# The second remainder in the split of B is made by GpSimd

## The chip, the cores and the metric

The kernel runs on one core of one Trainium2 chip. The metric is the time of one execution on the device in microseconds (us), as a median of several runs. A core has TensorE (PE in the profile, its weight loads PEld), VectorE (DVE), ScalarE (ACT), GpSimd (POOL) and SyncE (SP), which here only issues DMA transfers. Each engine works through its own queue in order; semaphores hold an instruction until the work of another engine that it needs is done.

## The reference

Four layers follow each other on four images of 64 x 64 positions and 96 channels. The first two are selective scans, the last two a linear attention with a small feed-forward part in quantised arithmetic. Nearly all of the time is in the first two. Of one of these, cut to what matters:

```python
x_dbl = jnp.einsum('bkdl,kcd->bkcl', xs, x_proj_weight)          # 4 directions k of each image
dts, Bmat, Cmat = jnp.split(x_dbl, [DT_RANK, DT_RANK + D_STATE], axis=2)
delta = jax.nn.softplus(jnp.einsum('bkrl,kdr->bkdl', dts, dt_projs_weight) + bias)
def step(h, inp):                                                # along l, 4096 positions
    u_l, dl, b_l, c_l = inp
    dA = jnp.exp(dl[..., None] * A)
    h = dA * h + (dl * u_l)[..., None] * b_l[:, :, None, :]      # 192 channels x 16 states
    y = jnp.einsum('bkdn,bkn->bkd', h, c_l)
    return (h, y)
```

B is a row for each of the 16 states, shared by all channels. Each channel's scan of state n needs the product of delta, u and B's row n.

## The kernel before

The images are taken in pairs. For each layer and pair, `scan_pair` runs four directions, in each four chunks of T = 1024 positions, and in each chunk three steps j: the first 128 channels of image 0, those of image 1, and a shared step (j = 2) with the last 64 channels of both. A step has 16 states, in eight groups of NG = 2. So a pair has 48 steps, the whole run 192, with 3072 scans of 128 x 1024.

For a group, ScalarE makes `da` = exp(delta x A) a group ahead (`start_ahead`). The product du x B comes in one of three ways, which the strings OWN and SHARED choose for each state. V: TensorE spreads B's row over 128 partitions into PSUM (`bp`, two buffers) with a selection matrix `sel`, and VectorE multiplies by `du`. A: ScalarE makes the product with time on the partitions (`x`), and TensorE turns it. G: GpSimd multiplies `du` by a copy of B that a transfer has spread (`dbu`), and the exponential goes to PSUM. Then VectorE scans (lines 659 to 666), GpSimd copies the last states (line 672) and multiplies each `h` by C (`cb`, line 674), and TensorE adds up over the states in `yp`, three groups later (LAG).

All instructions of the loop go through the helper at line 71, which keeps the order of the program on each engine. So the order of the calls in Python is the order in each queue, and the profile gives line 71 for all of them; rows are told apart by their tiles.

The work that prepares the next chunk is written as generators. `project` makes B, C and the input of delta for the chunk to come, and `drive` lets it go on at fixed places: `yield 2, 10` means in step j = 2, after the scans of the group that starts with state 10. The matmul that spreads B (way V) takes bfloat16. To keep the precision, B is split into three bfloat16 parts whose sum is B: `parts[0]` is B rounded, `rest` = B - `parts[0]` is the first remainder, `parts[1]` is `rest` rounded, and `parts[2]` = `rest` - `parts[1]` is the second remainder (line 385). Tiles: `parts` is 128 x 8 x 3 x 32 in bfloat16 and `rest` 128 x 8 x 32 in float32, both in SBUF with one buffer. Both are used once in three steps. The places are:

- (2, 8): ScalarE copies B out of PSUM to `bt` and rounds it to `parts[0]`; VectorE makes `rest` from PSUM and `parts[0]`
- (2, 10): ScalarE rounds `rest` to `parts[1]`, and at the same place the second remainder is made
- (2, 12): TensorE turns the parts in eight transposes (`bpps`)
- (2, 14): ScalarE copies them to `bparts`, which the next chunk's V states read

The 64 uses of `project` are 60 inside the loops and four at the openings of the pairs, where the chain runs on its own. The last step of each pair prepares nothing.

Of the kernel before, what the change touches and what calls it, by code (L numbers as in the profile page):

```python
# [21 lines left out]
ALU = mybir.AluOpType  # L22
# [308 lines left out]
def scan_pair(tc, pk, cst, ident, u, first_weights, layer, pr):  # L331

    nc = InOrder(tc)
    par, amat, dsum, w, y = layer.par, layer.amat, layer.dsum, layer.w, layer.y[pr]
    with ExitStack() as stage:
# [17 lines left out]
        def project(k, uv):  # L353


            wx = weights[k][0]
            bparts = p2.tile([NP, T], BF16, name="bparts")
            cdt = p2.tile([NC, T], F32, name="cdt")
            crow = pd.tile([ND, T], F32, name="crow")
            bt = p2.tile([128, T // 128, 2 * NS], F32, name="bt")  # L360
            projected.append((uv, bparts, crow, cdt, bt))
            for hf in range(2):
                for j in range(3):
                    yield hf, 8 + 2 * j
                    if j == 0:
                        ps = pm.tile([NC, 512], F32, name="xps", tag="m1")
                    nc.tensor.matmul(ps, wx[:, j], uv[j][:, 8 * hf : 8 * hf + 8], start=(j == 0), stop=(j == 2))
                yield hf, 14
                nc.scalar.copy(cdt[:, 512 * hf : 512 * hf + 512], ps)
            nc.sync.dma_start(out=crow, in_=cdt[:ND])  # L370
            yield 2, 6
            ps = pm.tile([128, T // 128, 2 * NS], F32, name="btps", tag="m1")
            for t in range(T // 128):
                nc.tensor.transpose(ps[:, t], cdt[BR, 128 * t : 128 * t + 128], ident[BR, BR])

            parts = p2.tile([128, T // 128, 3, 2 * NS], BF16, name="parts", bufs=1)
            rest = p2.tile([128, T // 128, 2 * NS], F32, name="rest", bufs=1)
            yield 2, 8
            nc.scalar.copy(bt, ps)
            nc.scalar.copy(parts[:, :, 0], ps)  # L380
            nc.vector.tensor_tensor(rest, ps, parts[:, :, 0], ALU.subtract)
            yield 2, 10
            nc.scalar.copy(parts[:, :, 1], rest)
            yield 2, 10
            nc.vector.tensor_tensor(parts[:, :, 2], rest, parts[:, :, 1], ALU.subtract)
            yield 2, 12
            ps = pm.tile([NP, T], BF16, name="bpps", tag="m1")
            for t in range(T // 128):
                nc.tensor.transpose(
                    ps[:, 128 * t : 128 * t + 128], parts[:, t].rearrange("p s n -> p (s n)"), ident16  # L390
                )
            yield 2, 14
            nc.scalar.copy(bparts, ps)
            yield None
# [46 lines left out]
        def begin_project(k, ci):  # L441
            tr, c = chunk_of(k, ci)
            return project(k, [part(t, tr, c) for t in u])
# [549 lines left out]
```

## Time and profile before

| | |
|---|---|
| time, median of 3 runs | 10827.77 us (10821.13 to 10835.91) |
| span of the profiled execution | 10818.7 us |
| granted TensorE clock, mean | 0.886 |
| scan loops of the four pairs | about 2300 to 2309 us each, 9214 us in all |
| scans on VectorE | 3072, 2.3 us each |
| multiplies of h by C on GpSimd | 3072, 2.37 us each |
| second remainder on VectorE | 64, 1.35 us each on average |

The scan loops are 85% of the span. Busy shares of the whole run mix them with the stages between the pairs and with the last two layers, so a stretch of a loop is what to read. A row of a group gives the engine, the operation, the tiles written and read, the shape and the number, then busy time and the mean of one. Idle time before an instruction is put down to the work that ended last before it.

### The profile page before, as it was taken

How to read it: one execution, taken by the hardware profiler on the slowest of the kernel's cores; microseconds unless marked ns; L12 is line 12 of the kernel's file. 1: busy time of each engine (PE TensorE's matmuls, PEld its weight loads, DVE VectorE, ACT ScalarE, POOL GpSimd, SP SyncE). 2: the span in 40 equal slices, each digit the busy share in tenths (PEclk: the TensorE clock that was granted, in tenths of full speed). 3: DMA queues.
4: the chain of work that ended last, by engine and by line, in shares of the span. 5: the costliest groups of instructions: out<-in, count | busy, mean ns of one | idle time of the engine just before them, and what ended most of it. 6: DMA issues, size and time to landing. Idle time of an engine off the chain costs nothing. (4 is left out here: it accounts for less than half of the span.)

```text
span 10818.7 us, 143079 instructions
## 1 busy us (share of the span) xinstructions
PE 8073.8 (75%) x48032; PEld 5963.0 (55%) x48032; DVE 9699.3 (90%) x6962; ACT 8758.7 (81%) x18679; POOL 9001.7 (83%) x5242
## 2 busy tenths in 40 slices
PE   7777777777777777777777777777777777777666
PEld 4555555554555555555555555555455555555544
DVE  7999999997899999998799999999699999999655
ACT  6888888885888888886688888888588888888556
POOL 3999999992899999996599999999299999999544
PEclk9899899988898998998898999999899989898766
DMA  4677777775677777776577777777467777777600
GB/s 123 205 210 217 213 225 217 218 216 138 199 212 209 219 218 218 220 215 193 149 209 210 212 218 221 217 218 213 136 206 213 212 215 222 218 216 214 184 3 25
DMA packets 960471, 2114.16 MB, mean 195 GB/s; under 512 B 413526, under 2 KB 704664, under 8 KB 762008
## 3 DMA queue, kind: packets, MB, share of 16 engines
q1 hardware_dynamic: 959736, 2105.01, 67.7%
q8 instruction: 381, 6.24, 0.2%
q14 instruction: 354, 2.90, 0.1%
HBM read 1943.27 MB, written 161.48 MB: 195 GB/s over the span
## 5 line engine op out<-in xcount | busy, mean ns | idle before, releaser
L71 POOL TENSOR_TENSOR h<-h,cb 128x1024 f32<-128x1024 f32 x3072 | 7198.4, 2367 | 268.9 <-issue 77.4
L71 DVE TENSOR_TENSOR_SCAN h<-da,last,bp 128x1024 f32<-128x1024 f32 x2064 | 4735.9, 2335 | 132.2 <-PE bp L71 15.1
L71 ACT ACTIVATE x<-dut,bt 128x128 f32<-128x128 f32 x12288 | 3495.3, 370 | 0.8 <-PE bp L71 0.5
L71 PE MATMUL yp<-ident,h 128*128 128x128 f32 x24576 | 3324.6, 295 | 9.8 <-POOL h L71 9.8
L71 PEld LDWEIGHTS yp<-ident,h 128*128 128x128 f32 x24576 | 3151.3, 155 | 126.4 <-issue 75.4
L71 ACT ACTIVATE da<-delta,amat 128x1024 f32<-128x1024 f32 x2752 | 3063.9, 1138 | 173.1 <-DVE h L71 172.9
L71 PE MATMUL bp<-ident,x 128*128 128x128 f32 x10240 | 1652.4, 312 | 1319.9 <-DVE h L71 920.8
L71 PEld LDWEIGHTS bp<-ident,x 128*128 128x128 f32 x10240 | 1333.4, 160 | 1880.0 <-ACT x L71 1046.2
L71 DVE TENSOR_TENSOR bp<-du,bp 128x1024 f32<-128x1024 f32 x1472 | 1779.2, 1213 | 230.3 <-PE bp L71 228.2
L71 DVE TENSOR_TENSOR_SCAN h<-da,bp 128x1024 f32<-128x1024 f32 x688 | 1537.7, 2274 | 48.8 <-ACT da L71 8.1
L71 PE MATMUL bp<-bparts,sel 96*128 96x512 bf16 x2944 | 922.5, 396 | 831.4 <-DVE h L71 810.4
L71 PEld LDWEIGHTS <-sel 96*128 96x128 bf16 x2944 | 224.3, 100 | 1640.5 <-DVE h L71 1030.3
L71 ACT ACTIVATE bp<-delta,amat 128x1024 f32<-128x1024 f32 x320 | 358.1, 1119 | 536.9 <-DVE h L71 535.5
L71 POOL TENSOR_TENSOR dbu<-du,bb 128x1024 f32<-128x1024 f32 x320 | 754.9, 2359 | 0.0
L71 POOL TENSOR_TENSOR du<-delta,u 128x1024 f32<-128x1024 f32 x192 | 506.8, 2640 | 202.3 <-ACT delta L71 176.5
L81 POOL TENSOR_TENSOR ln_rs<-ln_ve,half 128x4 f32<-128x4 f32 x64 | 83.9, 1311 | 596.0 <-DVE ln_ve L79 494.6
L71 DVE TENSOR_TENSOR_SCAN h<-bp,last,dbu 128x1024 f32<-128x1024 f32 x240 | 558.7, 2328 | 16.8 <-POOL dbu L71 13.1
L71 PE MATMUL xps<-u,wx 128*76 128x512 f32 x768 | 561.0, 820 | 5.7 <-ACT cdt L71 2.9
L71 POOL COPY last<-h 128x2 f32<-128x2 f32 x1152 | 223.0, 194 | 396.3 <-DVE h L71 394.4
L71 ACT ACT_TABLE_LOAD x384 | 492.7, 1283 | 7.1
L71 PE MATMUL dps<-cdt,wdt 12*128 12x512 f32 x768 | 448.0, 664 | 0.1
L71 ACT COPY dut<-dups 128x512 f32<-128x512 f32 x384 | 220.9, 575 | 255.0 <-PE dups L71 255.0
(132 smaller groups left out, 6439.4 us busy)
## 6 DMA issues: line engine op xcount, KB each, us to landing
cb<-crow SPq DMA_DIRECT2D x1024, 1024.0 KB
cb<-crow SPq DMA_DIRECT2D x1024, 512.0 KB
bb<-crow SPq DMA_DIRECT2D x384, 256.0 KB
bb<-crow SPq DMA_DIRECT2D x128, 512.0 KB
y<-ysum SPq DMA_DIRECT2D x192, 256.0 KB
kept<-y SPq DMA_DIRECT2D x160, 256.0 KB
y<-ysum SPq DMA_DIRECT2D x64, 512.0 KB
zt<-zg SPq DMA_DIRECT2D x64, 384.0 KB
```

The source lines that it names most:

```text
L71: return self.tc.keep_in_program_order(getattr(self.engine, op)(*args, **kwargs))
L81: nc.gpsimd.tensor_tensor(rs, ve, half, ALU.pow)
```

## The change

The second remainder, `parts[2]`, is subtracted by GpSimd rather than VectorE. The place in the program stays the same, and so do the tiles. It is meant to take a short instruction, and the wait ahead of it, out of VectorE's queue. In GpSimd's queue it stands after the multiplies of the group before (states 8 and 9) and ahead of the copy and the multiplies of states 10 and 11. The order on TensorE and ScalarE is as before.

```diff
             nc.scalar.copy(parts[:, :, 1], rest)
             yield 2, 10
-            nc.vector.tensor_tensor(parts[:, :, 2], rest, parts[:, :, 1], ALU.subtract)
+            nc.gpsimd.tensor_tensor(parts[:, :, 2], rest, parts[:, :, 1], ALU.subtract)
             yield 2, 12
```

## The prediction

> **What bounds the kernel now.** I read the page's first part, then the waits of each engine, then the stretch of one scan pair, then the two remainders themselves. The page's chain of waits is of no use here: its shares add up to 5% of the span, all in the attention and feed-forward layers at the end, so it never reaches the scans. First the page, the share of the span that each engine is busy:
>
> ```profile
> PE 8073.8 (75%) x48032; PEld 5963.0 (55%) x48032; DVE 9699.3 (90%) x6962; ACT 8758.7 (81%) x18679; POOL 9001.7 (83%) x5242
> ```
>
> Busy times by stretch, here the scan loop of the first image pair (the other three pairs have 2302 to 2309 us and the same loads within 0.3%):
>
> ```profile
> 180.00:2480.00 2300.00, 1726.12 (x10630) 1307.87 (x10630) 2182.34 (x1161) 1976.18 (x4244) 2143.85 (x1180) 0.90 0.75 214
> ```
>
> The columns are PE, PEld, DVE, ACT, POOL. In the loop VectorE is busy 94.9%, GpSimd 93.2%, ScalarE 85.9%. VectorE leads and GpSimd is close behind, so who waits for whom decides:
>
> ```profile
> DVE bp L71 <- PE bp L71: 228.2, 262, 11.8
> ...
> DVE rest L71 <- ACT parts L71: 56.5, 4, 24.5
> ...
> DVE parts L71 <- ACT parts L71: 52.0, 52, 1.5
> ...
> DVE h L71 <- POOL dbu L71: 28.0, 27, 1.8
> ```
>
> ```profile
> POOL last L71 <- DVE h L71: 394.4, 279, 11.8
> ```
>
> VectorE waits for GpSimd 28 us in the whole run; GpSimd waits for VectorE's scans 394 us. So the scans on VectorE set the pace, and what is taken out of VectorE's queue in the loop is worth nearly its time. The instructions on the tiles of the split (min, median, max in ns):
>
> ```profile
> L71 DVE TENSOR_TENSOR rest<-btps,parts x64: 396/399/426, 154.1 to 9956.7; 128x256 f32<-128x256 f32 x64
> L71 ACT CAST parts<-rest x64: 385/389/406, 154.5 to 9963.8; 128x256 bf16<-128x256 f32 x64
> L71 DVE TENSOR_TENSOR parts<-rest,parts x64: 424/1096/3250, 155.0 to 9964.5; 128x256 bf16<-128x256 f32 x64
> ```
>
> Both subtractions have the same 128x256 shape, but the second takes up to eight times the first. One instance in order of time, VectorE and then GpSimd:
>
> ```profile
> 440.75 2.33 DVE L71 TENSOR_TENSOR_SCAN h<-bp,last,dbu 128x1024 f32<-128x1024 f32 x1
> 444.41 2.46 DVE L71 TENSOR_TENSOR parts<-rest,parts 128x256 bf16<-128x256 f32 x1 [1.33 <-ACT parts L71]
> 446.80 1.22 DVE L71 TENSOR_TENSOR bp<-du,bp 128x1024 f32<-128x1024 f32 x1
> ```
>
> ```profile
> 443.97 0.18 POOL L71 COPY last<-h 128x2 f32<-128x2 f32 x1
> 444.23 4.87 POOL L71 TENSOR_TENSOR h<-h,cb 128x1024 f32<-128x1024 f32 x2
> 452.70 0.18 POOL L71 COPY last<-h 128x2 f32<-128x2 f32 x1 [3.60 <-DVE h L71]
> ```
>
> VectorE ends scan 11 at 443.08, waits 1.33 us for ScalarE's cast, and then the subtraction lies in its record for 2.46 us while GpSimd multiplies. GpSimd then idles 3.60 us, waiting for the scans that came late.
>
> **What the Trainium skill says.** "SBUF — State Buffer", section "Who interferes with whom": a VectorE instruction with two inputs in SBUF contends with a GpSimd instruction that reads SBUF, one with at most one SBUF input does not. The trace agrees: the first remainder (one input in PSUM) never exceeds 426 ns; the second (both in SBUF) takes 424 ns in the four openings, where GpSimd is idle, and 1.41 us on average in the loop. VectorE's other work in the loop has one input in PSUM: du by bp, and the scans, which read da or dbu beside bp. "GPSIMD Engine Reference", "Elementwise — side-by-side cycle accounting": 4497 ns for a two-input fp32 instruction of 2048 elements, 2.20 ns each; the trace's 1024-element multiply has 2367 ns, 2.31 each. "Perfetto Trace Analysis", "Optimizing Scalar/DVE Operations": offloading between these two engines might not help because of the shared port; here the contended operation is the very one that moves.
>
> **The change, part by part.**
>
> Removed from VectorE: 64 subtractions, 86.1 us by their group row (1345 ns mean). Four are in the openings of the pairs, where nothing else runs (4 x 0.42 = 1.7 us). The 60 in the loop are 84.4 us, or 1.41 each. The wait ahead of them goes too: 52.0 us, 0.87 each. An instruction's record reaches about 0.07 us into the next one (444.41 + 2.46 - 446.80), so 1.41 + 0.87 - 0.07 = 2.21 us each, 132 us. A second way gives the same: from the start of scan 11 to the start of scan 12 the 60 steps take 5.72 us on average, and the last step of each pair, which prepares no projection, takes 3.55 us four times out of four. 2.17 x 60 = **130 us**, which I use.
>
> What VectorE meets when it arrives 2.2 us earlier: its next work, du by bp for state 12, needs bp from TensorE. That buffer was freed by scan 10 at 443.0 - 2.3 = 440.8, and the two matmuls ran then. In the last steps of the pairs VectorE does go straight on. da for states 12 and 13 is on ScalarE ahead of the cast. So nothing stands directly behind the removed instruction.
>
> Given back later: the loop has 60 stalls of different size (0.43 to 4.5 us), a small experiment of its own. Regressing the time from state 12 to state 0 of the next step on the size of the stall gives -0.13 us for each us: a longer stall is partly made up, mostly at states 13 to 14, where VectorE waits for TensorE's bp. A whole step later the slope is -0.3, but with noise of 1.2 us. Around three more steps later it is lost in the noise. I take 18% given back: 130 x 0.82 = 107 us.
>
> Added to GpSimd: 64 subtractions of 256 elements. The trace has none on GpSimd. Lower bound 256 x 2.20 = 0.56 us from the page of the skill; upper 1.2 us, if the 2-byte, strided operand doubled the 0.59 us that 2.31 ns give. I take 0.7 us, the 0.59 plus part of the 0.27 us from the start of the small copy to the next multiply. In the loop 60 x 0.7 = 42 us. It comes ahead of the copy of the last states and the two multiplies of states 10 and 11. It waits for the cast, which ends 0.74 us after scan 11 on average; GpSimd reaches that point 0.86 us after scan 11 on average, so the wait is seldom over 1 us, and mostly where GpSimd would otherwise wait for scan 11. Behind it are the two multiplies, for which TensorE's adding-up waits three groups later. Today GpSimd starts the first of them 2.4 us on average after scan 11; with 0.7 more it lags about 3 us. A group costs it 0.19 + 2 x 2.37 = 4.9 us, VectorE 5.8 (state 12, 13) and 6.9 (14, 15), so the lag is gone by the next step. On the whole, a pair's GpSimd load becomes 2144 + 15 x 0.7 = 2155 us of about 2273, 95%. It stays off the path, and I cost it at **nothing**; VectorE's scans hide it.
>
> Moved: TensorE's eight transposes of parts wait for GpSimd rather than VectorE. They are queued ahead of bp for states 14 and 15. Today they start 5.4 us after scan 11 on average, and never under 3.2; GpSimd ends at about max(0.74, 0.86) + 0.7 = 1.6 us after scan 11, at worst about 3. Hidden behind TensorE's earlier work in its queue (the sums and the transposes of du), at no cost. The copy to bparts follows as before.
>
> The four openings: 0.7 instead of 0.42 us in a serial chain, 4 x 0.3 = +1 us. Outside the scans nothing changes. Sum: -107 + 1 = -106, **10,722 us**, -1.0%.
>
> **The rivals.**
>
> *All of it stays* (no give-back): 10,828 - 130 + 1 = 10,699. For it: the last steps of the pairs show 3.55 us exactly. Against: the slope.
>
> *Half is lost.* GpSimd at 95% has spikes: the step of the shared channels has three dbu products, 16 x 2.37 + 3 x 2.36 + 2.64 + 8 x 0.19 = 49 us of GpSimd, against 50.9 from start to start now and 48.8 once the stall is gone. If its lag grows until dbu comes late or TensorE's queue stands behind parts, about 1 us of each 2.2 comes back: 10,828 - 60 = 10,768. Against: the next two steps have one dbu each, 44 us against 46.2 and 46.8 from start to start.
>
> *No change:* ScalarE (86%) becomes the pace, because its casts, 16 scalings and table loads are what VectorE waited for at the cast. 10,828. Against: ScalarE itself waits 535 us for scans to free bp.
>
> *Slower:* the wait for the cast holds GpSimd at the head of its queue, the lag passes to TensorE, which stands at the transposes of parts with bp of states 14 and 15 behind, and VectorE loses 3 us where it gained 2.2: 60 x 0.8 = 48, 10,876. Against: 5.4 - 1.6 = 3.8 us of margin on average.
>
> **How the numbers follow.** The forecast with its give-back 0.58, all stays 0.12, half lost 0.17, no change 0.05, slower 0.08. The likeliest gives 10,722. The range goes from 10,688 (132 us and a few tenths of a per cent of measuring noise and idle) to 10,782 (half lost, with GpSimd's subtraction at 1.2 us): what is left out below and above is under 2 in 10. Faster by over 0.2%: 0.87; within: 0.05; slower: 0.08.
>
> **What would show it.** VectorE's busy time down by 86 us, its wait for ScalarE's parts down to the 56 us of the first remainder. Scan 11 to scan 12 in the shared step at about 3.55 us. Sixty GpSimd subtractions of 0.6 to 1.2 us; GpSimd's wait for scans down from 394 us. A scan loop of about 2275 us. Wrong if GpSimd's record is well over 1.2 us, if VectorE's wait for dbu or bp grows by more than 25 us, or if TensorE now waits for parts.

## The result and the profile after

The changed kernel takes 10,766.4 us (median of 6 runs, 10,753.4 to 10,773.7) against 10,826.5 us before (6 runs). The ratio is 0.9943, with a 95% interval of 0.9931 to 0.9956: 60 us less. The direction is as forecast and the size a little over half of the 106 us. Each experiment below has its ratio to runs of the kernel before that were made with it (medians of 10,823 to 10,826 us), so a difference of a few us between two experiments says nothing.

First the page after, the busy share of each engine:

```profile
PE 8109.9 (75%) x48032; PEld 6016.2 (56%) x48032; DVE 9622.5 (89%) x6898; ACT 8754.9 (81%) x18679; POOL 9028.9 (84%) x5306
```

VectorE lost 77 us of busy time and 64 instructions, GpSimd gained 27 us. The row of the second remainder in the view of the tile (min, median, max in ns):

```profile
L71 POOL TENSOR_TENSOR parts<-rest,parts x64: 661/673/695, 153.2 to 9908.1; 128x256 bf16<-128x256 f32 x64
```

On GpSimd it is 0.68 us, evenly. The waits of VectorE after the change (us in total, times, longest), and the one of GpSimd that answers to that shown before:

```profile
DVE bp L71 <- PE bp L71: 301.9, 332, 13.1
...
DVE rest L71 <- ACT parts L71: 53.9, 4, 24.5
...
DVE h L71 <- POOL dbu L71: 24.1, 23, 2.1
```

```profile
POOL last L71 <- DVE h L71: 338.3, 238, 11.8
```

The wait for the cast is gone from VectorE's list; what is left of ScalarE's parts there is the first remainder in the four openings. VectorE's wait for GpSimd's dbu did not grow (28.0 to 24.1). But its wait for TensorE's bp rose from 228.2 to 301.9 us, and that is the surprise. The instance shown before, now in the changed kernel, on VectorE:

```profile
438.03 2.34 DVE L71 TENSOR_TENSOR_SCAN h<-bp,last,dbu 128x1024 f32<-128x1024 f32 x1
440.29 1.21 DVE L71 TENSOR_TENSOR bp<-du,bp 128x1024 f32<-128x1024 f32 x1
441.60 4.59 DVE L71 TENSOR_TENSOR_SCAN h<-da,last,bp 128x1024 f32<-128x1024 f32 x2
446.91 2.36 DVE L71 TENSOR_TENSOR bp<-du,bp 128x1024 f32<-128x1024 f32 x2 [0.73 <-PE bp L71]
```

and on GpSimd:

```profile
442.82 0.68 POOL L71 TENSOR_TENSOR parts<-rest,parts 128x256 bf16<-128x256 f32 x1
443.44 0.19 POOL L71 COPY last<-h 128x2 f32<-128x2 f32 x1
443.71 4.69 POOL L71 TENSOR_TENSOR h<-h,cb 128x1024 f32<-128x1024 f32 x2
448.35 0.18 POOL L71 COPY last<-h 128x2 f32<-128x2 f32 x1
```

After scan 11 VectorE goes straight on. Four instructions later, at the product for state 14, it waits 0.73 us for TensorE. GpSimd works without a gap.

Where the time went is read best from the start of one scan to the start of the next. I took these from the scan rows of the timeline and averaged over all 64 steps of a kind. The profile also records which share of its full clock TensorE was granted; "half clock" is the time in records of 0.5, per step, between the starts of those states (in the last row over the 60 places where a step follows inside the same pair).

| | before | after | change x 64 |
|---|---|---|---|
| shared step, scan 11 to 12 | 5.59 us | 3.56 us | -130 us |
| shared step, 13 to 14 | 4.57 us | 5.23 us | +42 us |
| next step (image 0), 1 to 2 | 4.33 us | 4.70 us | +24 us |
| step of image 1, 1 to 2 | 3.94 us | 4.09 us | +10 us |
| four scan loops in all, first scan's start to last scan's end | 9224 us | 9175 us | -50 us in all |
| half clock, states 11 to 14 of the shared step | 6.72 us | 6.60 us | |
| half clock, state 15 to state 2 of image 0's step | 4.61 us | 6.68 us | |

The 130 us came as forecast. 76 of them were given back at three places, all of them waits for TensorE. The profiled spans differ by 57 us; the 7 us that are not in the loops have no cause that I know.

### The profile page after: what moved, and what is told of

Its sections match the earlier page's. It is cut to its first block, busy times and chain, and to the rows that moved or that the text cites. A ratio compares the mean times of both kernels' runs of the same rounds, so it can differ in the third digit from the quotient of the medians.

```text
span 10761.8 us, 143139 instructions
## 1 busy us (share of the span) xinstructions
PE 8109.9 (75%) x48032; PEld 6016.2 (56%) x48032; DVE 9622.5 (89%) x6898; ACT 8754.9 (81%) x18679; POOL 9028.9 (84%) x5306
## 5 line engine op out<-in xcount | busy, mean ns | idle before, releaser
L71 PE MATMUL bp<-ident,x 128*128 128x128 f32 x10240 | 1679.8, 316 | 1288.9 <-DVE h L71 938.7
L71 PEld LDWEIGHTS bp<-ident,x 128*128 128x128 f32 x10240 | 1361.0, 163 | 1852.8 <-ACT x L71 1025.7
L71 DVE TENSOR_TENSOR bp<-du,bp 128x1024 f32<-128x1024 f32 x1472 | 1780.6, 1214 | 303.3 <-PE bp L71 301.9
L71 ACT COPY ysum<-yp 128x1024 f32<-128x1024 f32 x192 | 194.4, 1012 | 288.9 <-PE yp L71 288.9
```

What stands on the lines that cost most here:

```text
L71: return self.tc.keep_in_program_order(getattr(self.engine, op)(*args, **kwargs))
```

## Experiments

**Does GpSimd take it back?** Nothing makes the third part any more; it is zeroed once for each pair.

```diff
         weights = {0: first_weights}
+        parts = p2.tile([128, T // 128, 3, 2 * NS], BF16, name="parts", bufs=1)
+        nc.gpsimd.memset(parts, 0.0)
...
-            nc.gpsimd.tensor_tensor(parts[:, :, 2], rest, parts[:, :, 1], ALU.subtract)
```

> Leaves the second remainder out on both engines: the third part of B is set to zero once for each pair and never made again, so the output is slightly less precise and the time shows what the subtraction on GpSimd costs. Theory TensorE (what came back after the change, +0.66 us at states 13 to 14 and +0.37 us at states 1 to 2 of the next step, is TensorE's queue, which starts at half clock): the time stays at 10,760 to 10,770 us, within 5 us of the changed kernel. Rival GpSimd (the 0.7 us in GpSimd's queue, and its wait for the cast, delay the multiplies and what waits for them): about 40 to 49 us less, 10,720 us.

10,767.7 us, ratio to before 0.9949 (0.9936 to 0.9961), the same as the changed kernel. States 13 to 14 take 5.26 us and states 1 to 2 of image 0's step 4.70, as with the subtraction. So the subtraction on GpSimd, and the order that it forces there, cost nothing that these runs can tell, and the rival GpSimd falls.

**Was it the shared port?** In the kernel before, `rest` moves from SBUF to PSUM, into one tile with B.

```diff
-            ps = pm.tile([128, T // 128, 2 * NS], F32, name="btps", tag="m1")
+            both = pm.tile([128, 2, T // 128, 2 * NS], F32, name="btps", tag="m1")
+            ps, rest = both[:, 0], both[:, 1]
...
-            rest = p2.tile([128, T // 128, 2 * NS], F32, name="rest", bufs=1)
```

> The kernel before, with the second remainder still on VectorE, but with the first remainder kept in PSUM, so that the subtraction has one input in SBUF only. Theory shared port (the time over 0.42 us was contention with GpSimd): its record falls from 1.35 us to 0.42 to 0.5 us on average, the wait for the cast stays at about 50 us in all, scan 11 to scan 12 falls from 5.7 to about 4.8 us, and the time falls by 40 to 60 us, to about 10,775 us. Rival (the long records have another cause, such as the strided 2-byte operand or a late semaphore): the record stays over 1 us and the time within 10 us of before.

The rows of the two remainders in the view of the tile, where `btps` is now B and `rest` together:

```profile
L71 DVE TENSOR_TENSOR btps<-btps,parts x64: 405/406/433, 153.8 to 9921.0; 128x256 f32<-128x256 f32 x64
L71 DVE TENSOR_TENSOR parts<-btps,parts x64: 396/425/426, 154.7 to 9928.5; 128x256 bf16<-128x256 f32 x64
```

The same subtraction of the same shape, still on VectorE, into the same strided 2-byte tile, falls from up to 3250 ns to 426 ns at most. So what was long was the second SBUF input beside a busy GpSimd, as the Trainium skill's "SBUF — State Buffer" ("Who interferes with whom") states. Its wait for the cast stays (46.6 us in 44 times). Scan 11 to 12 takes 4.58 us, and states 13 to 14 stay at 4.61, so nothing is given back there; states 1 to 2 of the next two steps give back 18 us. The time is 10,771 us, 0.9949 (0.9937 to 0.9962): this edit removes one of the two microseconds of the stall and brings about as much as the change that removes both. So the second microsecond is worth little. How little stays open: 5 us by the medians, 16 by the loops of the two profiled executions (9191 and 9175 us), and that of this edit was the slowest of its five.

**What holds TensorE up?** TensorE's queue between bp for state 13 and bp for state 14, before and then after the change:

```profile
443.23 1.94 PE L71 MATMUL bp<-ident,x 128*128 128x128 f32 x8 [1.30 <-DVE h L71]
444.96 3.08 PE L71 MATMUL yp<-ident,h 128*128 128x128 f32 x16
447.88 0.60 PE L71 MATMUL dups<-ident,du 128*128 128x128 f32 x4
448.32 0.61 PE L71 MATMUL bpps<-ident,parts 128*96 128x128 bf16 x8
450.45 0.60 PE L71 MATMUL bp<-bparts,sel 96*128 96x512 bf16 x2 [1.53 <-DVE h L71]
```

```profile
440.51 1.94 PE L71 MATMUL bp<-ident,x 128*128 128x128 f32 x8 [1.37 <-DVE h L71]
442.25 3.31 PE L71 MATMUL yp<-ident,h 128*128 128x128 f32 x16
445.39 0.60 PE L71 MATMUL dups<-ident,du 128*128 128x128 f32 x4
445.83 0.61 PE L71 MATMUL bpps<-ident,parts 128*96 128x128 bf16 x8
446.28 1.03 PE L71 MATMUL bp<-bparts,sel 96*128 96x512 bf16 x4
```

Before, TensorE came to bp for state 14 and waited 1.53 us for VectorE; after, it goes straight through, and VectorE waits for it. Both chains begin at the end of scan 11, which frees the buffer for bp 13. Averaged over the 60 places, in us after that moment:

| | before | after |
|---|---|---|
| TensorE: bp 13 done | 2.09 | 2.09 |
| sums done | 5.08 | 5.09 |
| transposes of du done | 5.58 | 5.56 |
| bp 14 starts | 6.28 | 5.85 |
| VectorE: scan 13 done | 7.96 | 5.79 |
| scan 14 starts | 10.22 | 8.75 |

TensorE's work did not move by more than 0.02 us up to the transposes of du. VectorE used to come 1.7 us after bp 14 had started, and now comes 0.06 us before it starts. The stretch is slow in TensorE because it begins at half clock: 16 transposes of the sums take 3.1 to 3.3 us here, and 1.91 us at full clock. Over the whole changed kernel these transposes, within a run, follow each other every 213 ns inside records of 0.5 and every 109 ns inside records of 1.0. Ahead of the stretch TensorE idles in the group with state 11, whose bp ScalarE makes, until bp for state 12 (here after the change):

```profile
438.17 0.97 PE L71 MATMUL bp<-bparts,sel 96*128 96x512 bf16 x2 [3.28 <-DVE h L71]
```

The Trainium skill, "TensorE: Matmul & The Clock Gate", "What's actually happening", says that the throttled clock is the default and that activity releases it. The trace agrees, and the length of a single pause is not what counts. The clock records here hold 1.0 and 0.5 and change on a grid of 3.41 us. In the loops of the changed kernel each of the 347 returns to 1.0 came after a stretch of the grid in which TensorE was busy for at least 78.7%, each of the 343 falls to 0.5 after one of at most 77.9%, and every stretch under 45% was followed by 0.5. To test what the clock is worth, extra matmuls with unused results fill that idle time:

```diff
             nc.gpsimd.tensor_tensor(parts[:, :, 2], rest, parts[:, :, 1], ALU.subtract)
+            warm = pm.tile([128, 512], F32, name="warm", tag="m1")
+            for _ in range(8):
+                nc.tensor.matmul(warm, sel[:, 0, :128], sel[:, 0:2], start=True, stop=True)
```

> The changed kernel, with eight extra 128x512 bfloat16 matmuls (results unused) in TensorE's queue at the place of the second remainder, where TensorE otherwise idles 3.3 us before bp of state 12. Theory TensorE's clock: the half-clock stretch at states 11 to 13 goes, the 16 transposes of the sums there run at full clock, states 13 to 14 fall from 5.23 to about 4.5 to 4.7 us, and the time falls by 30 to 55 us, to about 10,725 us. Rival queue length alone (TensorE simply has more work between bp 13 and bp 14 than VectorE): the clock changes but states 13 to 14 stay over 5 us and the time is within 10 us. Rival GpSimd: no change.

10,742.2 us, 0.9927 (0.9914 to 0.9939), 24 us less than the changed kernel. Half clock in states 11 to 14 falls from 6.60 to 3.66 us, bp 14 starts at 5.49 rather than 5.85 us, and states 13 to 14 take 4.96, 17 us in all. This is less than expected: the clock is part of it, not all, and over half of the half-clock time is still there. The other part is the length of the queue:

```diff
             nc.gpsimd.tensor_tensor(parts[:, :, 2], rest, parts[:, :, 1], ALU.subtract)
-            yield 2, 12
+            yield 2, 14
             ps = pm.tile([NP, T], BF16, name="bpps", tag="m1")
```

> The changed kernel with TensorE's eight transposes of the parts moved from after state 12's group to after bp of states 14 and 15. Theory TensorE (whatever stands between bp 13 and bp 14 in its queue delays VectorE): states 13 to 14 fall by about 0.5 us, the length of the eight transposes, and the time by 20 to 35 us, to about 10,740 us. Rival ScalarE: its copy to bparts now waits for the later transposes, the exponentials of the next step come late, and the gain comes back as a wait of states 0 to 2 of the next step; time within 10 us. Rival GpSimd: no change at states 13 to 14.

10,763.2 us, 0.9942 (0.9929 to 0.9956). States 13 to 14 fall to 4.94 us, bp 14 starts at 5.51 us, but image 0's next step lost 0.54 us: the product x of its state 1 is ready 2.78 us after scan 15 rather than 1.80, and its states 13 to 14 take 4.42 rather than 3.99 us. The step of image 1 gained 0.33, so that little is left of it all. The rival ScalarE was right on the time, but not on the place: states 1 to 2 of image 0's step did not grow (4.66 us against 4.70). What links the late x to the loss at states 13 to 14 is not shown. Both edits together:

> The changed kernel with both edits: the eight extra matmuls at the place of the second remainder, and the transposes of the parts after bp of states 14 and 15. Theory TensorE (queue from scan 11 to bp 14, anchored at the end of scan 11): bp 14 starts at about 5.1 us after scan 11 rather than 5.85, before VectorE ends scan 13 at 5.79, so states 13 to 14 are back at 4.5 us, and none of the first give-back is left. The copy to bparts still makes the product x of the next step's state 1 late, as with the later transposes alone, so the time is about 10,735 to 10,745 us. Rival (a fixed cost elsewhere, such as da of state 14 on ScalarE): states 13 to 14 stay at 4.9 us.

10,728.6 us, 0.9912 (0.9898 to 0.9925), somewhat better than expected. bp 14 starts at 4.84 us and states 13 to 14 take 4.63 us. The first give-back is gone, as expected: clock and length of TensorE's queue make it up.

**The second give-back.** After the change TensorE does bp 14, bp 15 and their sums in one run and then idles 2.6 us until the next step. A second set of extra matmuls goes there (`keep_warm` holds the three lines shown above; the transposes stay where the change has them):

```diff
             nc.gpsimd.tensor_tensor(parts[:, :, 2], rest, parts[:, :, 1], ALU.subtract)
+            keep_warm()
...
             nc.scalar.copy(bparts, ps)
+            keep_warm()
             yield None
```

> The changed kernel with the eight extra matmuls at two places: the place of the second remainder, and after the copy to bparts, where TensorE idles 2.6 us before the next step's first bp. Theory clock (the second give-back, +0.37 us at states 1 to 2 of the next step, is TensorE at half clock there): half clock in states 15, 0 and 1 falls from 6.9 us to under 4 us, states 1 to 2 of the step for image 0 fall from 4.70 to 4.3 us or less, and the time falls to about 10,715 to 10,725 us. Rival (x of state 1 from ScalarE sets it): unchanged at 4.7, time as with one place, 10,742 us.

TensorE at the head of image 0's step, in the changed kernel:

```profile
451.67 0.79 PE L71 MATMUL bp<-bparts,sel 96*128 96x512 bf16 x2 [2.61 <-DVE h L71]
453.91 1.94 PE L71 MATMUL bp<-ident,x 128*128 128x128 f32 x8 [1.45 <-DVE h L71]
455.64 3.44 PE L71 MATMUL yp<-ident,h 128*128 128x128 f32 x16
```

and with the extra matmuls at both places:

```profile
450.45 1.89 PE L71 MATMUL warm<-sel 96*128 96x512 bf16 x8
453.05 0.60 PE L71 MATMUL bp<-bparts,sel 96*128 96x512 bf16 x2 [0.71 <-DVE h L71]
455.38 1.07 PE L71 MATMUL bp<-ident,x 128*128 128x128 f32 x8 [1.72 <-DVE h L71]
456.28 1.91 PE L71 MATMUL yp<-ident,h 128*128 128x128 f32 x16
```

The same work, 3.44 us and 1.91 us. Half clock from state 15 to state 2 falls from 6.68 to 1.81 us and states 1 to 2 from 4.70 to 3.73 us, below the 4.33 of the kernel before. The time is 10,689.6 us, 0.9876 (0.9862 to 0.9889), 77 us less than the changed kernel, more than expected: the best version. Its loops are 97 us shorter than those of the changed kernel, but the stages ahead of them are some 20 us longer. The extra matmuls also run in the four openings, where the chain runs alone and the second set stands ahead of the matmuls for delta: from the first remainder to the first scan of the pair the openings take 82.7 us in all, 61.1 in the changed kernel. Leaving them out there should bring about 20 us more; that is an estimate from these two sums, and no run shows it.

**Is it the clock, or the clock where nothing covers it?** The extra matmuls at the first place, in the kernel before:

> The kernel before, with VectorE's second remainder, and the eight extra matmuls at its place. Theory (in the kernel before, VectorE's stall of 2.2 us covers TensorE's slow stretch): scan 11 to scan 12 stays at 5.6 us and states 13 to 14 at 4.57, the time falls by 10 us at most, although the half-clock time falls as in the changed kernel. Rival (a faster TensorE clock is worth the same in either kernel): 20 to 25 us less than before, about 10,800 us.

10,833.7 us, ratio 1.0008 (1.0000 to 1.0016): no gain. Half clock in states 11 to 14 falls to 4.19 us, yet states 13 to 14 stay at 4.55. VectorE's stall hid TensorE's slow stretch. Then at both places in the kernel before:

> The kernel before, second remainder on VectorE, with the eight extra matmuls at both places. Tells how much of the gain with two places belongs to the change. Theory: at states 11 to 14 nothing is gained (VectorE's stall covers TensorE there, as with one place), at the head of the next step the extra matmuls help as they did in the changed kernel, from 4.33 to about 3.7 us, 36 us for the step of image 0 and up to 15 us for that of image 1; so about 10,775 to 10,790 us. The change is then worth about 90 us with TensorE kept at full clock, against 60 us without. Rival (the stall spreads TensorE's work so that there is nothing to gain): within 10 us of before.

10,780.6 us, 0.9960 (0.9948 to 0.9972), as expected: states 1 to 2 fall to 3.70 us, states 13 to 14 stay at 4.63. With the extra matmuls at both places states 1 to 2 of image 0's step are alike before and after the change (3.70 and 3.73 us, against 4.33 and 4.70 without them), so the second give-back there is gone. The change is now worth 10,780.6 - 10,689.6 = 91 us, against 60 without them. By the intervals of the two ratios the 91 is uncertain by about 20.

**Two more attempts.** Extra matmuls also in the groups with state 7 and at the start of the shared step:

```diff
                 sum_of(g - LAG)
+            if n0 == 6 or (j == 2 and n0 == 0):
+                keep_warm()
```

> As with the two places, and extra matmuls also in every group that holds state 7 and in the first group of the shared step, where a state of way G leaves TensorE without a bp to make. An attempt at a faster version. Theory clock: the half-clock stretch at states 1 to 3 of the shared step goes, states 3 to 4 there fall from 4.46 to about 3.7 us, and the time falls by a further 20 to 50 us, to about 10,680 to 10,700 us. Rival: the extra matmuls themselves hold up bp, or other half-clock stretches appear, and the time is no better than with two places.

10,777.6 us, 0.9959 (0.9946 to 0.9971), 88 us worse than with two places. The half-clock time in all stays at 2093 us (2683 in the changed kernel). States 7 to 8 rise from 3.54 to 4.19 us (image 0) and from 3.64 to 4.54 (shared), and states 13 to 14 are back at 5.21. That the extra matmuls stand ahead of the next bp where there is no room is the likely cause. And, against the theory, states 3 to 4 of the shared step stay at 4.3 us (4.36 with two places), though half clock from the start of state 1 to that of state 4 falls from 5.9 to 4.6 us: that wait has another cause, which I leave open.

The transposes moved, and the extra matmuls at both places:

> The changed kernel with the extra matmuls at both places and the transposes of the parts after bp of states 14 and 15. Theory: states 13 to 14 fall from 4.92 with two places to 4.6, 19 us in all, but the copy to bparts, and behind it x of state 1, are late, since ScalarE waits for the transposes, and take back about as much at states 1 to 2; time 10,680 to 10,705 us. Rival (queue of TensorE alone counts): 10,670 us.

10,704.6 us, 0.9890 (0.9877 to 0.9902). States 13 to 14 gain 0.15 us, x of state 1 is late as before (2.80 us), and the sum is 15 us worse. The rival, TensorE's queue alone, forecast 10,670 us and falls. The loss appears later in image 0's step (12 us at states 3 to 4, 13 at 6 to 7, 11 at 13 to 14), not at states 1 to 2, which gained 9; that ScalarE's queue is behind it is likely, not shown.

## Why the prediction was right, and where it was not

- **What is removed.** 130 us was forecast and 130 us came at scan 11 to 12, to 3.56 us, the figure of the steps without a projection.
- **Port and wait.** The stall was told as contention plus a wait for the cast. Moving `rest` to PSUM showed the first by itself: 1.35 us to 0.42 on average.
- **GpSimd at nothing.** 0.7 us was taken, 0.68 measured. Leaving it out changed nothing that shows. GpSimd's load in the first loop's stretch rose to 2149 of 2300 us and stayed off the path. One reading was wrong: GpSimd ends the multiplies of states 8 and 9 not 0.86 but 1.84 us after scan 11 on average, so that its subtraction ends at 2.84 us (3.21 at most), not at 1.6. The margin was smaller than thought, and still enough.
- **The transposes of parts, hidden.** They were: TensorE reached them at the same time after scan 11 as before (5.40 and 5.41 us).
- **The failed term: "Given back later", 18%, 23 us.** It measured 76 us in the loops, over half. The sign and the place of its first part (states 13 to 14, TensorE's bp) were right. The size came from a straight line through stalls from 0.43 to 4.5 us, carried on to none. But the relation has a bend. TensorE needs about 6.5 us after scan 11 for bp 14, whose two matmuls start at 5.85 and take 0.6 together; VectorE arrives at 5.79 us plus the stall. A stall above some 0.7 us hides TensorE entirely, and only below does the wait appear. The trace of before held this: of the 13 places with the smallest stall, six show 5.4 to 5.6 us from 13 to 14; the other seven and all 47 places with longer stalls show 4.4 to 4.6. Those 13 should have been read apart.
- **What no step foresaw.** The second part, 24 + 10 us at states 1 to 2, goes with more half-clock time, 6.68 us for 4.61: with TensorE's work in one run, the pause after it is 2.6 us on average where it was 2.2. The prediction treated TensorE's durations as fixed. For image 0's step the extra matmuls at both places, put into both kernels, showed the clock as the cause; for the 10 us of image 1 it is not shown.
- **The rivals.** "Half is lost" gave 10,768 and has the right number, for a reason that does not hold: it was no lag of GpSimd (VectorE's wait for dbu fell from 28.0 to 24.1 us), and TensorE did not stand behind parts. The range reached up to 10,782 for the sake of this rival alone, so that the measured 10,766 lies in it is luck in part: the forecast's own sum was 44 us too low. "Slower" failed since GpSimd had the subtraction ready 2.6 us before TensorE came to it, on average. ScalarE as the pace showed up only where an edit made its queue wait.
- **The signs named ahead.** The rise of VectorE's wait for bp by more than 25 us (74) was named as a sign that the prediction is off, and it was. The other signs came: the wait for ScalarE's parts is down to 53.9 us, GpSimd's wait for scans to 338. VectorE's busy time fell by 77 us rather than 86, and a loop takes 2289 to 2305 us rather than 2275.

## What to carry to other kernels

Before counting the whole of a removed stall, follow the next engine from the moment when its chain is released, and ask when it would be ready without the stall: the gain ends there. Read the cases with the smallest stall by themselves, not through a line over all. And a short operation with two SBUF inputs beside a busy GpSimd could be mended here by moving one input to PSUM, for about the same gain as by moving the operation.

## What the hardware showed that was not expected

TensorE fell to half clock with pauses of only 2.2 to 3.3 us between runs of work, and the same 16 transposes then took 3.44 rather than 1.91 us. What told the falls from the returns was the busy share of a 3.41 us stretch, with the divide between 77.9% and 78.7% in the loops of the changed kernel, though not every stretch between 45% and the divide was followed by a fall. Sixteen unused matmuls for each projection, well placed, took 77 us off the changed kernel at nearly the same busy time of TensorE in the first loop (1745 us of 2268 against 1740 of 2300); placed in further groups as well, they cost 88 us again. In the openings, where nothing hides them, the sixteen cost some 20 us.
